# Last chunks, recurrence start and final checks of a convolution-attention-recurrence kernel: matmul before scaling, spread roots, and a hinted branch

## The chip, the cores and the metric

The kernel runs on one core of one Trainium2 chip. The metric is the device time in microseconds (us) of one execution; lower is better. The core's engines each work through their own queue in order: TensorE (PE in the profile, with its weight loads as PEld), VectorE (DVE), ScalarE (ACT), GpSimd (POOL) and SyncE (SP, which here only issues DMAs). They wait for each other through semaphores.

## The reference

The input x has 8 images of 128 channels and 48 x 48 pixels, so 2304 positions. All arithmetic is float32. Two layers are computed:

```
# layer 0: causal attention over the positions
x0 = concat(group_norm(x), position_rows)            # 128 + 32 channels
q, k, v = leaky_relu(W? @ x0 + b?)                   # three times 128 x 2304
x = x + softmax(mask(q.T k / sqrt(128))) v
# layer 1: t = x as tokens, (8, 2304, 128)
n = layer_norm(t);  t = t + softmax(n n.T) n         # full attention
n = layer_norm(t)                                    # over the 128 channels
w = batch_norm(n @ W.T)                              # mean, variance over all 8 * 2304 tokens
y = 0;  for each position: y = sigmoid(w[position] + y @ V.T)
out = t + all the y
```

The batch norm needs every token of all images before the first step of the recurrence. The recurrence is serial over 2304 positions in the reference.

## The kernel before, in words

Positions go through the kernel in chunks of QC = 384, six to an image (`j` = 0 to 5), each of QB = 3 blocks of 128. For every image `b`, class `Causal` computes layer 0's attention and class `Full` layer 1's. `Full` uses that its score matrix is symmetric: a block of exponentials computed for one chunk is turned over by VectorE, stored to DRAM and loaded again for a later chunk (the "turned" products of L1329, from tiles `g`), so that only part of the scores are multiplied out ("direct", L1316 and L1341); the small mirrored ones within a chunk are at L1337.

**How the order is set.** Everything is scheduled by hand. The list `stream` holds all the scores and products in order; each product comes LAG = 3 items behind its score. Beside it a planner (class `Stream`) holds chains of steps. A step is a triple: its function, the TensorE time that it takes, and a list of engine times that says when the next step of its chain falls due; an entry with an empty name is plain waiting time. The planner's clock `now` counts matmul time. After each item `tick` runs at most two steps that are due. A step that needs another chain to be further on forces it with `advance` or `finish`, due or not. So a step's place in each engine's queue follows from these due times, and an engine that reaches a step too early simply waits.

**What follows a chunk of `Full`** (method `after`, L1349): ScalarE copies the chunk's result out of PSUM (`of`, L1361). `residual` transposes it (`of_t`), divides by the softmax sums (`dn`, `ri`), adds the residual into `t2` and computes the token means and variances (`mv`, `ve`). `rooted` has POOL compute the inverse roots. Then there are two ways.

- All chunks but the last two of the last image: the turned `t2` and the turned roots go to DRAM (`spread`), and come back laid out by channel (`fetch`: `t2x` at L1416, and the roots spread over all partitions as `scale` at L1418). `product` keeps `t2x` in `t2c`, multiplies raw `t2x` by the weight `w1T` (L1424), and multiplies the result by the roots (L1425). The weight's rows were centred at the start, so the mean of layer norm needs no subtraction. `stored` copies the result to `wx` (L1430).
- Chunks 4 and 5 of the last image (`last`): `keep_last` transposes `t2` back on TensorE (`tk`, L965) and copies it to `t2c` (L1445); `normed` normalises the tokens on VectorE (L952); `back` transposes them (`tx`) and ScalarE copies them (`xc`, L1460); `statistics` multiplies by `w1T` (L1464), takes statistics (L1469) and copies to `wx` (L1470).

`keep` fills one half of `t2c` with each chunk, and before that forces the chain of the chunk before it; `store` then writes a full `t2c` to DRAM. For chunk 5, `after` also finishes chunk 4's chain and aggregates the statistics so far (L1367). Between these steps `idle` puts matmuls into TensorE's queue whose results nobody reads (L1505); each of its calls is two instructions in the profile.

**The recurrence** (from L1558). The 2304 positions are cut into 96 segments of LS = 24, and all segments of all images run side by side; each starts with WARM = 10 extra steps taken from the segment before, so that its state has converged. The segments form G = 3 groups. Per step and group, TensorE adds `vT_f` times the last state to the input in PSUM tile `z` (L1666), and ScalarE applies the sigmoid (L1667). VectorE makes the inputs two steps at a time as a times wx plus c (`inputs`, L1611, from the batch norm's coefficients `bn_a` and `bn_c`), and the first step's state comes straight from `wx` (L1669). `add_residual` adds `t2` to two steps of states and has SP write them out (L1646, L1647); POOL does it for the second and third group up to a point, VectorE for what is left, and group 0's first 16 steps are written by an accumulating DMA (L1682). The adds' output buffers `rlast` are 8.

**The end.** `seams` (L1632) compares each segment's last state with the state that the next segment's extra steps had reached, `off` says whether any differs too much, and `fl` says whether the attention's scores could have grown too large. A matmul (L1697) and an addition (L1698) make `flag` of both. All engines load it (L1711) and branch (L1712): over `general_path`, the slow and general program, or into it.

Of the kernel before, what the change touches and what calls it, by code (L numbers as in the profile page):

```python
# [14 lines left out]
F32 = mybir.dt.float32  # L15
# [589 lines left out]
def fast_path(ctx: ExitStack, tc: tile.TileContext, x, pe, w_ffn, out, x_tok, w_qkv, w_pos, v_t, gamma_beta, flag):  # L605
# [52 lines left out]
    gb = cpool.tile([P, 2], F32, tag="gb", name="gb")  # L658
    half = cpool.tile([P, 1], F32, tag="half", name="half")
    nc.gpsimd.memset(half, 0.5)  # L660
    v_half = cpool.tile([P, 1], F32, tag="v_half", name="v_half")
    gbv = cpool.tile([P, 1], F32, tag="gbv", name="gbv")

# [7 lines left out]
    with ExitStack() as actx:  # L671
# [16 lines left out]
        def psum_s(name):  # L688
            return ps_s.tile([P, CH], F32, tag="s", name=name)
# [6 lines left out]
        def chunk_tile(tag, name, holder=None, steps=0, bufs=2):  # L696

            if holder is not None:
                before = holders.setdefault(tag, deque([({}, 0)] * bufs))
                old, n = before.popleft()  # L700
                before.append((holder, steps))
                if "chain" in old:
                    st.advance(old["chain"], n)
            return (work if bufs == 2 else work1).tile([P, QC], F32, tag=tag, name=name)
# [245 lines left out]
        def normalize(dst, y, mv, rs):  # L950
            for g in range(QB):
                nc.vector.tensor_scalar(dst[:, ts(g, P)], y[:, ts(g, P)], mv[:, g, 0:1], rs[:, g : g + 1], ALU.subtract, ALU.mult)  # L952
# [7 lines left out]
        def turned_back(src, name):  # L960

            tp = psum_t(name)
            out_ap = tp[:, :QC].rearrange("p (a g r) -> p g a r", a=R, g=QB)
            for g in range(QB):
                nc.tensor.transpose(out_ap[:, g], src[:, ts(g, P)], ident)  # L965
            return tp
# [218 lines left out]
        class Full:  # L1185
# [163 lines left out]
            def after(self, j, o):  # L1349
# [79 lines left out]
                    store()  # L1429
                    nc.scalar.copy(wx[:, :, b, ts(j, SJ)], c["scale"].rearrange("p (s l) -> p l s", l=LS))  # L1430

                def normed():
                    c["x2"] = chunk_tile("t2x", f"x2_{b}_{j}", c, 5, bufs=1)
                    normalize(c["x2"], c["t2"], c["mv"], c["rs"])

                before = self.before.get("chain")

                def keep(t2x):

                    k = j % (SG // SJ)  # L1440
                    if before is not None:
                        st.advance(before, 6 if k else len(before.steps) + before.done)
                    if k == 0:
                        self.t2c = work1.tile([P, LS, SG], F32, tag="t2c", name=f"t2c_{b}_{j}")
                    nc.scalar.copy(self.t2c[:, :, ts(k, SJ)], t2x.rearrange("p (s l) -> p l s", l=LS))  # L1445
# [8 lines left out]
                        nc.sync.dma_start(out[0, :, :LA, b, :], self.t2c[:, :LA])  # L1454
                        nc.sync.dma_start(t2l_d[:, :, b, :], self.t2c[:, LA:])

                def back():
                    tp = turned_back(c["x2"], f"tx_{b}_{j}")
                    c["xc"] = chunk_tile("scale", f"xc_{b}_{j}", c, 6, bufs=1)
                    nc.scalar.copy(c["xc"], tp[:, :QC])  # L1460

                def statistics():
                    tp = psum_t(f"wx_{b}_{j}")
                    nc.tensor.matmul(tp[:, :QC], w1T, c["xc"], start=True, stop=True)  # L1464
                    to = stats[:, b * NQ + j, :]
                    if b == B - 1 and j == NQ - 1:
                        idle(psum_s("idle_last2"), 8)
                        to = most[:, 3:]
                    nc.vector.bn_stats(to, tp[:, :QC])  # L1469
                    nc.scalar.copy(wx[:, :, b, ts(j, SJ)], tp[:, :QC].rearrange("p (s l) -> p l s", l=LS))  # L1470

                def keep_last():
                    keep(turned_back(c["t2"], f"tk_{b}_{j}")[:, :QC])
                    if b == B - 1 and j == NQ - 1:
                        idle(psum_s("idle_last1"), 8)
                    store()

                if last:
                    steps = [
                        (keep_last, 0.35, [("ACT", 0.85)]),  # L1480
                        (normed, 0.0, [("DVE", 1.1)]),
                        (back, 0.35, [("ACT", 0.5)]),
                        (statistics, QC * US, [("DVE", 0.55), ("ACT", 0.85)]),
                    ]
                else:
                    steps = [
                        (turn_root, 0.0, [("DVE", 0.15)]),
                        (spread, 0.0, [("", 13.0)]),
                        (fetch, 0.0, [("", 12.0)]),
                        (product, QC * US, [("DVE", 1.0)]),  # L1490
                        (stored, 0.0, [("ACT", 0.85)]),
                    ]
                c["chain"] = self.before["chain"] = st.add([
                    *through,
                    (residual, 0.0 if far else 0.35, [("DVE", 4.0)]),
                    (rooted, 0.0, [("POOL", 0.9)]),
                    *steps,
                ], max(at, st.free["DVE"]) + 0.2 - st.now)

# [2 lines left out]
        def idle(tp, n):  # L1502

            for _ in range(n):
                nc.tensor.matmul(tp[:, :P], ident, ident, start=True, stop=True)  # L1505
# [57 lines left out]
    with ExitStack() as rctx:  # L1563
# [23 lines left out]
        for t in range(-WARM, -WARM + 2 * TZ, TZ):  # L1587
            for g in range(G):
                z = ps_z[g].tile([P, TZ, B, SG], F32, tag="z", name=f"z_{g}_{t}")
                nc.tensor.matmul(z.rearrange("p t b s -> p (t b s)"), zero[:, :P], zero, start=True, stop=True)  # L1590
                banks[g].append(z)
        idle(pw[:, 2 * P :], 8)

        mv = rc.tile([P, 2], F32, tag="bn_mv", name="bn_mv")
        nc.vector.bn_aggr(mv, most)
# [43 lines left out]

        ys = {}  # L1640

        def add_residual(g, l0, yt):
            engine, pool = (nc.gpsimd, rres) if g and l0 < LM - TZ else (nc.vector, rlast)
            r = pool.tile([P, TZ, B, SG], F32, tag="r", name=f"r_{g}_{l0}")
            t2 = t2s[g].rearrange("p b l s -> p l b s")[:, l0 : l0 + TZ] if g else t2l[:, l0 - LA : l0 - LA + TZ]
            engine.tensor_add(r, yt, t2)  # L1646
            nc.sync.dma_start(out[g, :, l0 : l0 + TZ], r)  # L1647


        nc.tensor.matmul(pw[0:1, :B], ones[:, 0:1], bound, start=True, stop=True)  # L1650
        fl = rc.tile([1, 4], F32, tag="fl", name="fl")
        nc.vector.reduce_max(fl[:, 0:1], pw[0:1, :B], AX.X)
        nc.vector.tensor_scalar(fl[:, 1:2], fl[:, 0:1], LOGIT_BOUND / SCALE, None, ALU.is_gt)
# [32 lines left out]
                    for l0 in range(LA, LM, TZ):  # L1686
                        add_residual(0, l0, ys[0, l0])

        for l0 in range(LM, LS, TZ):
            for g in range(G):  # L1690
                add_residual(g, l0, ys[g, l0])
        for g in range(G):
            seams(g)
        off = rc.tile([P, 1], F32, tag="off", name="off")
        nc.vector.tensor_reduce(off, dm, AX.X, ALU.max)
        nc.vector.tensor_scalar(off, off, STATE_TOL, None, ALU.is_gt)
        nc.tensor.matmul(pw[0:1, P : P + 1], off, ones[:, 0:1], start=True, stop=True)  # L1697
        nc.vector.tensor_scalar(flag, pw[0:1, P : P + 1], fl[:, 1:2], 0.5, ALU.add, ALU.is_gt)  # L1698

@with_exitstack
def conv_attn_hybrid_kernel(ctx: ExitStack, tc: tile.TileContext, args, laid):


    nc = tc.nc
    fpool = ctx.enter_context(tc.tile_pool(name="flag", bufs=1))
    flag = fpool.tile([1, 1], mybir.dt.int32, tag="flag", name="flag")
    x, w_ffn, pe, out = (args[i] for i in (0, 7, 11, 12))
    fast_path(tc, x, pe, w_ffn, out, *laid, flag)  # L1710
    redo = nc.values_load(flag[0:1, 0:1], min_val=0, max_val=1, skip_runtime_bounds_check_because="the flag is the result of a comparison")  # L1711
    with tc.If(redo > 0):  # L1712
        general_path(tc, *args)


# [39 lines left out]
```

## Time and profile before

| what | value |
|---|---|
| three runs | 1713.53, 1719.08 and 1719.97 us; median 1719.08 |
| the profiled execution | 1715.02 us, of which the span from first to last instruction is 1713.3 |
| instructions | 22451 |
| busy in the span | PE 1687.8 us (99%), DVE 1209.1 (71%), ACT 684.8 (40%), POOL 449.9 (26%) |
| mean granted TensorE clock | 0.995 |
| DMA | 291.67 MB, mean 170 GB/s |

Busy times are those of single instructions on the engine; a matmul's end is modelled. The parts that the change touches are all in the last 90 us of the span: the last image's chunks 4 and 5 (from about 1620 us), the coefficients of the batch norm (around 1650 us), the recurrence's 34 steps (to 1698 us) and the end. The profile describes one execution, and the runs are others.

### The profile page before, as it was taken

How to read it: one execution, taken by the hardware profiler on the slowest of the kernel's cores; microseconds unless marked ns; L12 is line 12 of the kernel's file. 1: busy time of each engine (PE TensorE's matmuls, PEld its weight loads, DVE VectorE, ACT ScalarE, POOL GpSimd, SP SyncE). 2: the span in 40 equal slices, each digit the busy share in tenths (PEclk: the TensorE clock that was granted, in tenths of full speed). 3: DMA queues.
4: the chain of work that ended last, by engine and by line, in shares of the span. 5: the costliest groups of instructions: out<-in, count | busy, mean ns of one | idle time of the engine just before them, and what ended most of it. 6: DMA issues, size and time to landing. Idle time of an engine off the chain costs nothing.

```text
span 1713.3 us, 22451 instructions
## 1 busy us (share of the span) xinstructions
PE 1687.8 (99%) x6259; PEld 1085.4 (63%) x6259; DVE 1209.1 (71%) x3297; ACT 684.8 (40%) x1300; POOL 449.9 (26%) x637
## 2 busy tenths in 40 slices
PE   9999999999999999999999999999999999999986
PEld 5666666666666666666666666666666666666665
DVE  5875578666886578865787568865798657974467
ACT  3344334433344324443244333443244442443355
POOL 1233122312133122322124112331213221341205
PEclk9999999999999999999999999999999999999998
DMA  3337763568445774368735684448743686347857
GB/s 122 101 89 210 225 200 109 131 193 251 129 129 145 238 230 128 79 189 244 205 101 130 199 252 139 125 130 244 227 146 71 176 244 207 81 96 211 237 221 223
DMA packets 316731, 291.67 MB, mean 170 GB/s; under 512 B 195793, under 2 KB 280690, under 8 KB 315956
## 3 DMA queue, kind: packets, MB, share of 16 engines
q1 hardware_dynamic: 306572, 268.76, 54.7%
q0 software_dynamic: 9792, 20.99, 4.5%
q8 instruction: 52, 0.85, 0.2%
q14 instruction: 83, 0.68, 0.1%
q10 hardware_dynamic: 232, 0.40, 0.1%
HBM read 164.13 MB, written 125.90 MB: 169 GB/s over the span
## 4 chain that ended last, share of the span: by engine, by line
PE 96%; DMA 2%; DVE 1%; SPq 0%; issue 0%; ACT 0%; DVEq 0%; ACTq 0%
PE s L1038 17%; PE s L1316 17%; PE o L1049 17%; PE o L1341 17%; PE o L1329 13%; PE pj L899 3%; PE pj L902 2%; PE o L1337 2%; PE z L1666 2%; PE wx L1424 2%; DMA g<-e 1%; PE of_t L957 1%; PE pb L847 0%; PE idle_last L1505 0%; DMA x<-in_x_dram 0%; DMA e<-t 0%
## 5 line engine op out<-in xcount | busy, mean ns | idle before, releaser
L1318 ACT ACTIVATE p<-s,shift 128x384 f32<-128x384 f32 (+2 forms) x504 | 274.2, 550 | 535.9 <-PE s L1316 436.8
L1040 ACT ACTIVATE p<-s 128x384 f32<-128x384 f32 (+2 forms) x504 | 229.4, 460 | 400.1 <-PE s L1038 323.6
L1038 PE MATMUL s<-q,k 128*128 128x384 f32 (+2 forms) x1008 | 380.6, 459 | 0.1
L1316 PE MATMUL s<-xh 128*128 128x384 f32 (+2 forms) x1008 | 379.2, 458 | 0.0
L1049 PE MATMUL o<-p,vT 128*128 128x384 f32 (+2 forms) x1008 | 377.5, 456 | 0.0
L1341 PE MATMUL o<-p,xhT 128*128 128x384 f32 (+2 forms) x1008 | 369.1, 456 | 0.0
L1281 DVE STREAM_TRANSPOSE t<-p 128x384 f32<-128x384 f32 x360 | 186.0, 553 | 170.8 <-DMA e<-t 106.3
L1329 PE MATMUL o<-g,xhT 128*128 128x384 f32 x720 | 282.2, 489 | 0.7 <-DMA g<-e 0.7
L1341 PEld LDWEIGHTS o<-p,xhT 128*128 128x128 f32 x1008 | 189.7, 190 | 120.3
L1049 PEld LDWEIGHTS o<-p,vT 128*128 128x128 f32 x1008 | 186.9, 190 | 109.9 <-POOL p L1043 2.0
L1316 PEld LDWEIGHTS s<-xh 128*128 128x128 f32 x1008 | 183.2, 191 | 99.6 <-issue 0.2
L1038 PEld LDWEIGHTS s<-q,k 128*128 128x128 f32 x1008 | 183.4, 190 | 99.0 <-issue 2.2
L1064 DVE TENSOR_TENSOR acc<-acc,p 128x384 f32<-128x384 f32 (+2 forms) x408 | 212.5, 521 | 23.1 <-DVE acc L1064 1.0
L1329 PEld LDWEIGHTS o<-g,xhT 128*128 128x128 f32 x720 | 132.6, 191 | 80.2 <-DMA g<-e 2.2
L1043 POOL TENSOR_TENSOR p<-p,triu 128x128 f32<-128x128 f32 x144 | 71.3, 497 | 356.1 <-ACT p L1040 355.8
L1266 POOL DMA_DIRECT2D gm<-m x192 | 105.3, 555 | 179.1 <-PE s L1316 63.2
L1262 POOL DMA_DIRECT2D m<-tm x48 | 29.9, 623 | 374.5 <-DVE tm L1249 374.5
L1138 POOL TENSOR_SCALAR xhT<-xhT 128x384 f32<-128x384 f32 x48 | 60.5, 1260 | 150.5 <-DVE yt L1150 121.2
L1249 DVE STREAM_TRANSPOSE tm<-p 128x256 f32<-128x256 f32 x96 | 33.9, 366 | 73.1 <-ACT p L1318 72.3
L899 PE MATMUL pj<-xn,wT 128*128 128x384 f32 x192 | 77.9, 488 | 1.5 <-DVE xn L892 1.5
L947 POOL TENSOR_TENSOR rs_c<-ve_c,mhalf 128x3 f32<-128x3 f32 x48 | 48.2, 1004 | 96.1 <-DVE ve_c L941 86.8
L906 DVE TENSOR_TENSOR q<-pj,pb 128x384 f32<-128x384 f32 x48 | 26.6, 554 | 50.1 <-PE pj L899 50.1
(256 smaller groups left out, 1681.1 us busy)
## 6 DMA issues: line engine op xcount, KB each, us to landing
e<-t SPq DMA_DIRECT2D x480, 144.0 KB
g<-e SPq DMA_DIRECT2D x120, 576.0 KB
pb<-posb_d SPq DMA_DIRECT2D x42, 576.0 KB
t1t<-in_x_tok_dram SPq DMA_DIRECT2D x48, 192.0 KB
m<-tm POOLq DMA_DIRECT2D x48, 192.0 KB, 4.3
gm<-m POOLq DMA_DIRECT2D x192, 48.0 KB, 3.8
t_d<-tt SPq DMA_DIRECT2D x184, 48.0 KB
t2x<-t_d SPq DMA_DIRECT2D x46, 192.0 KB
```

What stands on the lines that cost most here:

```text
L899: nc.tensor.matmul(ps[:, :QC], wT[:, j, :], xn, start=True, stop=True)
L1038: nc.tensor.matmul(s[:, off:QC], keys[b][:, ts(m, P)], queries[b, j][:, off:], start=True, stop=True)
L1040: nc.scalar.activation(p[:, off:], s[:, off:QC], AF.Exp, scale=SCALE)
L1043: nc.gpsimd.tensor_mul(p[:, off : off + P], p[:, off : off + P], triu)
L1049: nc.tensor.matmul(o[:, off:QC], vals[b][:, ts(m, P)], p[:, off:], start=first, stop=last)
L1064: nc.vector.tensor_add(a[:, off:], a[:, off:], p[:, off:])
L1266: nc.gpsimd.dma_start(gm[ts(r, SQ)].rearrange("c a q r -> c a (q r)"), d.rearrange("(a c) b f -> b c a f", a=R)[r])
L1281: nc.vector.transpose(t[:, :, :, g, :].rearrange("p b j r -> p j b r"), p.rearrange("p (j b r) -> p j b r", j=QB, b=R))
L1316: nc.tensor.matmul(s[:, off:QC], xh[:, ts(m, P)], xh[:, j * QC + off : (j + 1) * QC], start=True, stop=True)
L1318: nc.scalar.activation(p[:, off:], s[:, off:QC], AF.Exp, bias=shift)
L1329: nc.tensor.matmul(out_ap, xhT[:, QB * i + g, :], p, start=first, stop=last)
L1341: nc.tensor.matmul(o[:, off:QC], xhT[:, what[1], :], p[:, off:], start=first, stop=last)
```

## The change: what it does

1. `keep_last`, `raised`, `statistics` replace `keep_last`, `normed`, `back`, `statistics` for the two last chunks. `raised` multiplies `w1T` by the raw tokens in `t2c`, and ScalarE copies the product (`wr`). `statistics` spreads the three columns of roots over all partitions with three matmuls (a root column, broadcast, as the stationary operand, against the identity), VectorE multiplies product and roots in place and takes the statistics, and ScalarE copies to `wx`. The due times of chunk 4's steps get plain waiting time added: 5.0 us after `rooted`, 3.0 after `keep_last`, 1.0 after `raised`. Chunk 5's `idle` after `keep_last` has 4 calls instead of 8.
2. In chunk 5's `statistics` a sigmoid of one column (`scrap`) is issued before the copy to `wx`.
3. At the recurrence's start the 8 calls of `idle` go, and the matmul for `fl` takes their place, ahead of the coefficients.
4. At the end, the seams and `off` come first; of the six last additions of the residual, two (the last two steps of groups 0 and 1) are made by TensorE, which adds `t2` and the states in PSUM through the identity and leaves a copy to ScalarE; VectorE keeps the other four, one before the flag and three behind it.
5. The flag is inverted. A branch hint is placed on all engines before the flag is loaded, and the branch is written so that skipping `general_path` is the jump.

```diff
 # Full.after: steps of the two last chunks
                     if before is not None:
-                        st.advance(before, 6 if k else len(before.steps) + before.done)
+                        st.advance(before, min(6 if k else 7, len(before.steps) + before.done))
...
+                final = b == B - 1 and j == NQ - 1
+
+                def keep_last():
+                    keep(turned_back(c["t2"], f"tk_{b}_{j}")[:, :QC])
+                    if final:
+                        idle(psum_s("idle_last1"), 4)
+                    store()
+
+                def raised():
+                    tp = psum_t(f"wr_{b}_{j}")
+                    k = j % (SG // SJ)
+                    nc.tensor.matmul(
+                        tp[:, :QC].rearrange("p (l s) -> p l s", l=LS), w1T, self.t2c[:, :, ts(k, SJ)], start=True, stop=True
+                    )
+                    c["wr"] = chunk_tile("scale", f"wr_{b}_{j}", c, 5, bufs=1)
+                    nc.scalar.copy(c["wr"], tp[:, :QC])
 
                 def statistics():
                     tp = psum_t(f"wx_{b}_{j}")
-                    nc.tensor.matmul(tp[:, :QC], w1T, c["xc"], start=True, stop=True)
-                    to = stats[:, b * NQ + j, :]
-                    if b == B - 1 and j == NQ - 1:
+                    by_token = tp[:, :QC].rearrange("p (a g r) -> p g a r", a=R, g=QB)
+                    for g in range(QB):
+                        nc.tensor.matmul(by_token[:, g], c["rs"][:, g : g + 1].to_broadcast([P, P]), ident, start=True, stop=True)
+                    if final:
+                        nc.scalar.activation(scrap, half, AF.Sigmoid)
                         idle(psum_s("idle_last2"), 8)
-                        to = most[:, 3:]
-                    nc.vector.bn_stats(to, tp[:, :QC])
-                    nc.scalar.copy(wx[:, :, b, ts(j, SJ)], tp[:, :QC].rearrange("p (s l) -> p l s", l=LS))
...
+                    z = c["wr"].rearrange("p (l s) -> p l s", l=LS)
+                    nc.vector.tensor_mul(z, tp[:, :QC].rearrange("p (s l) -> p l s", l=LS), z)
+                    nc.vector.bn_stats(most[:, 3:] if final else stats[:, b * NQ + j, :], c["wr"])
+                    nc.scalar.copy(wx[:, :, b, ts(j, SJ)], z)
 
                 if last:
                     steps = [
-                        (keep_last, 0.35, [("ACT", 0.85)]),
-                        (normed, 0.0, [("DVE", 1.1)]),
-                        (back, 0.35, [("ACT", 0.5)]),
-                        (statistics, QC * US, [("DVE", 0.55), ("ACT", 0.85)]),
+                        (keep_last, 0.35, [("ACT", 0.85), ("", 0.0 if final else 3.0)]),
+                        (raised, QC * US, [("ACT", 0.5), ("", 0.0 if final else 1.0)]),
+                        (statistics, 0.35, [("DVE", 1.1), ("ACT", 0.85)]),
                     ]
...
-                    (rooted, 0.0, [("POOL", 0.9)]),
+                    (rooted, 0.0, [("POOL", 0.9), ("", 5.0 if last and not final else 0.0)]),
...
 # recurrence, start
-        idle(pw[:, 2 * P :], 8)
+        nc.tensor.matmul(pw[0:1, :B], ones[:, 0:1], bound, start=True, stop=True)
...
-        nc.tensor.matmul(pw[0:1, :B], ones[:, 0:1], bound, start=True, stop=True)
         fl = rc.tile([1, 4], F32, tag="fl", name="fl")
...
 # recurrence, end
-        for l0 in range(LM, LS, TZ):
-            for g in range(G):
-                add_residual(g, l0, ys[g, l0])
+        def summed(g, l0):
+
+            z = ps_z[g].tile([P, TZ, B, SG], F32, tag="z", name=f"zr_{g}_{l0}")
+            for part, start in ((tokens_of(g, l0), True), (ys[g, l0], False)):
+                nc.tensor.matmul(z, ident, part, start=start, stop=not start)
+            r = rlast.tile([P, TZ, B, SG], F32, tag="r", name=f"r_{g}_{l0}")
+            nc.scalar.copy(r, z)
+            return partial(nc.sync.dma_start, out[g, :, l0 : l0 + TZ], r)
+
+        summed(0, LS - TZ)()
         for g in range(G):
             seams(g)
         off = rc.tile([P, 1], F32, tag="off", name="off")
         nc.vector.tensor_reduce(off, dm, AX.X, ALU.max)
         nc.vector.tensor_scalar(off, off, STATE_TOL, None, ALU.is_gt)
+        store = summed(1, LS - TZ)
         nc.tensor.matmul(pw[0:1, P : P + 1], off, ones[:, 0:1], start=True, stop=True)
-        nc.vector.tensor_scalar(flag, pw[0:1, P : P + 1], fl[:, 1:2], 0.5, ALU.add, ALU.is_gt)
+        for g in range(G):
+            add_residual(g, LM, ys[g, LM])
+            if g == 0:
+                store()
+                nc.vector.tensor_scalar(flag, pw[0:1, P : P + 1], fl[:, 1:2], 0.5, ALU.add, ALU.is_le)
+        add_residual(2, LS - TZ, ys[2, LS - TZ])
 # the branch
-    redo = nc.values_load(flag[0:1, 0:1], min_val=0, max_val=1, skip_runtime_bounds_check_because="the flag is the result of a comparison")
-    with tc.If(redo > 0):
+    tc.mark_branch_hint_location("redo", "LikelyTaken", engines=list(nc.engines))
+    kept = nc.values_load(flag[0:1, 0:1], min_val=0, max_val=1, skip_runtime_bounds_check_because="the flag is the result of a comparison")
+    with tc.If(kept > 0, preferred_fallthrough_block=False, label="redo") as same:
+        pass
+    with same.Else():
         general_path(tc, *args)
```

## The prediction

> **What bounds the kernel now.** I read the page first. TensorE is busy 99% of the 1713.3 us, so in the attention loops only fewer or faster matmuls would help, and the change leaves those loops alone. What can move is the last 90 us, where the order of small steps decides. I went there with the timeline, then the waits, then the instructions of the branch.
>
> Waits from 1625 to 1656 us (engine and line, what it waited for: total, times, longest):
>
> ```profile
> PE wx L1424 <- DMA t2x<-t_d: 4.0, 1, 4.0
> ACT L1669 <- DVE bn_cv L1602: 1.3, 1, 1.3
> DVE fl L1652 <- PE pw L1650: 1.2, 1, 1.2
> ```
>
> The first is TensorE standing still in the last chunk of attention; the others sit at the start of the recurrence. The timeline (start, duration, engine, line, operation) gives the places:
>
> ```profile
> 1631.37 1.14 ACT L1445 COPY t2c<-t2x 128x384 f32<-128x384 f32 x1 [4.98 <-DMA t2x<-t_d]
> ...
> 1639.36 1.43 DVE L1367 BATCH_NORM_AGGREGATE most<-stats 128x2 f32<-128x282 f32 x1
> ...
> 1641.82 0.56 DVE L1376 TENSOR_REDUCE dn<-of_t 128x3 f32<-128x384 f32 x1 [0.78 <-PE of_t L957]
> ...
> 1644.74 0.49 PE L965 MATMUL tk<-ident,t 128*128 128x128 f32 x3
> ...
> 1649.63 0.20 DVE L1595 BATCH_NORM_AGGREGATE bn_mv<-most 128x2 f32<-128x9 f32 x1
> ...
> 1651.38 1.28 ACT L1669 ACT_TABLE_LOAD   x1 [1.32 <-DVE bn_cv L1602]
> ...
> 1654.44 0.80 DVE L1620 TENSOR_SCALAR z_-8_14609<-wx,bn_a,bn_c 128x512 f32<-128x512 f32 x1
> ```
>
> These rows are the milestones that I cost: t2x lands, `dn` starts the final residual, `bn_mv` closes the statistics, and the second input tile (`z_-8`) starts. After 1656.81 TensorE repeats every 0.43 us with no wait, so the recurrence shifts as a block with that tile. Its last sigmoid ends at 1698.06. What follows is 15.2 us of tail:
>
> ```profile
> 1704.67 0.21 DVE L1698 TENSOR_SCALAR flag<-pw,fl 1x1 int32<-1x1 f32 x1 [0.28 <-PE pw L1697]
> ```
>
> and, from the lists of instructions of lines 1712 and 1751 (times in ns, first and last start in us):
>
> ```profile
> L1712 PEldq COMPARE_BRANCH  x1: 3462/3462/3462, 1705.5 to 1705.5; - x1
> L1712 SPq EVENT_SEMAPHORE  x8: 17/17/17, 1709.2 to 1709.8; - x8
> L1751 POOLq DRAIN  x3: 46/107/2685, 1709.7 to 1713.0; - x3
> ```
>
> The flag is ready at 1704.88, all engines branch by 1705.6, none does anything before 1709.0, and GpSimd's 2.69 us drain comes last.
>
> **What the skill says.** "Runtime: NRT & Kernel Launch", section "Instruction fetch mechanics": a taken branch to a page outside the fetched window must wait for a DMA of that page. The 3.46 us above agrees. "ScalarE: Activation LUTs", "What ACT_TABLE_LOAD costs": about 1283 ns plus a drain of 1380 ns. Here the load takes 1.28 us and the sigmoid starts at 1652.67 directly behind it; no drain shows. "TensorE: Matmul & The Clock Gate", "What's actually happening": an idle window of about 3.4 us halves the clock. Here the 4.0 us stall is followed by a granted clock of 0.54 from 1633.0 to 1636.5, with products 0.64 us apart instead of 0.32.
>
> **Step 1, chunk 4 of the last image.** `keep_last` forces chunk 3's `product`, in whose matmul TensorE waits for t2x. `rooted` now gives 5 us more before it. The products behind that place are seven turned ones (0.645 us each), chunk 5's own scores and product (0.21 each) and one mirrored (0.22), 5.2 us: `keep_last` comes out one product before the end, and the stall goes. But t2x is fetched when t_d has landed (1625.9), untouched, so it still lands at 1631.37, and ScalarE's queue now decides. TensorE reaches chunk 3's matmul about 1633.0 (turned products wait some 0.4 us for their tile) and ends it at 1633.7. VectorE's product takes 0.56, and ScalarE's strided copy 1.14 (wx<-scale): 1635.6. The t2c store, next in line with about 2.4 us, lands earlier, at 1635.0. Then come copy tk 0.48 (1636.1), the raw product 0.9 cold (1637.05), the spread roots as three fp32 matmuls of 0.244 each (16 half ones of L1505 take 1.95 us) and 0.17 latency (1637.85), multiply 0.60, bn_stats 0.60 (1639.05), the aggregate 1.43 and two small ones 0.25: `dn` at 1640.8 instead of 1641.82. **Gain 1.0**, though the stall and slow clock were over 5 us. SP's order around the fetch does not change. The final o copy sits behind copy tk, ending at 1636.6, under this cover.
>
> **Step 2, final chunk.** `dn` to the root's end took 4.30 (1646.12) and stays. Then came normalise, transpose, copy, matmul, bn_stats: 3.51 until 1649.63. Now three spreads 1.0 with hops, multiply 0.60, bn_stats 0.65: 2.25. **Gain 1.25.** The raw product must be there first: t2 at `dn`+1.9, transposes 0.4, four idle calls 0.98 (ScalarE's copy beside them), product 0.8, copy 0.55 make `dn`+4.6; the multiply waits until `dn`+5.3. The 14 idle calls (3.4) end at 1641.7, ahead of t2 at 1642.7; now they delay tk by a microsecond.
>
> **Step 3, into the recurrence.** Scrap's sigmoid loads the table ahead of wx's copy, under VectorE's multiply and statistics; the first sigmoids follow `bn_cv` at once. The flag's matmul moves before the coefficients and eight idle calls (1.95) go, so VectorE passes `fl` in 0.3 us rather than waiting: from `bn_mv` to `z_-8` 3.67 instead of 4.81. **Gain 1.15.** ScalarE's own gain (1.3) and TensorE's (over 2) are larger, so VectorE decides. Together the recurrence starts 3.4 us sooner. The t2s loads start 1.8 sooner too, since tk does; POOL's adds and their outputs shift as one.
>
> **Step 4, tail**, in the old frame, before the shift. Six adds of 0.60 and a 0.45 wait preceded the seams. Now VectorE starts them at 1697.3; 2.6 us and two small ones give `off` at 1700.3. TensorE's four residual products, 512 columns or 0.853 each (twice z's 0.43), end at 1701.05, and the flag's matmul queues behind. Flag: 1701.5, not 1704.88. ScalarE's two copies (about 0.6) hide. Three of VectorE's adds remain behind the flag, to 1703.35, so SP issues its last write at 1703.4, 1.5 later than before, and branches at 1704.3, not 1705.46. POOL, idle, branches near 1702 and drains under this. The hint stands behind each engine's last work, so SP arms it only 0.5 us ahead: target at 1707.45 for 1709.22. Its semaphores take 1.42 as before, then 0.9 of barrier: 1709.8 for 1713.26. **Gain 3.45.**
>
> Sum: 1.0 + 1.25 + 1.15 + 3.45 = **6.9 us**. The profiled execution took 1715.02 (span 1713.3 plus 1.7), giving 1708.1. But the three runs lie at 1713.53, 1719.08 and 1719.97; the median of these four is 1717.05, which I take: **1710**.
>
> **Costs not shown.** A weight load with stride zero: nothing if like other loads (0.19), up to 0.5 if element fetch slows it; a better layout might gain 0.1; I take zero. The multiply reads PSUM at stride 24: L1470's ScalarE copy reads so at 0.48 without penalty; VectorE's could cost 0 to 0.6 (its contiguous z, unlike scale, could save ScalarE 0.66, off the path); I take zero. The hint: lost, minus 0.5; perfect, plus 2.5; its own instruction 0 to 0.1.
>
> **Rivals.** (A, 0.43) The sum above, 3.9 to 9.9. (B, 0.40) The target is there when the engines branch. SP's part would end near 1705.7; then the last write, issued 1703.4 and landing about 2.4 later like the t2c store, binds, with 1.4 of semaphores and barrier: 1707.2. Gain 9.4, **1707.6**. For it: five engines fetched in the same 4 us before and now arrive spread out. Against: SP's half microsecond. (C, 0.12) The wait only moves: t2c's store lands later or the strided multiply is slow, steps 1 and 2 give nothing, and a late write eats 1 us of the tail: gain 3.5, **1713.5**. This includes that the hint does nothing. (D, 0.05) Slower: TensorE is short of filler. It now idles from 1634.0 to 1636.2, 1.2 us before tk, and again around the roots; should the clock be half as the recurrence starts, each step costs 2.58 rather than 1.29. Six steps eat the gain; 16 steps give **1731**. Against: each gap is under the 4.0 that halved it before.
>
> **How the numbers follow.** A measurement here tells about 0.5% from no change, 8.6 us. B lies beyond it almost wholly (0.38), A by two fifths (0.17), C not: faster 0.55, same 0.40, slower 0.05. A's and B's spread and the base (1715 to 1719) give 1703; C sets 1716.
>
> **What would show it.** Right: no wait of TensorE for t2x near 1631, `dn` near 1640.8, the table load before `bn_mv`, `bn_mv` to `z_-8` under 3.8, flag 3.4 after the last sigmoid. Wrong: `dn` past 1641.8; a clock of half past `bn_mv`; SP's first semaphore behind the branch under 1 us (B) or 3.7 us after it (no hint). A recurrence pace other than 0.43 would overturn the sum.

## The result and the profile after

| what | before | after |
|---|---|---|
| median of 22 runs | 1716.55 us (1711.96 to 1721.94) | 1709.76 us (1707.72 to 1714.95) |
| the profiled execution, its span | 1715.02, 1713.3 us | 1714.05, 1712.0 us |

The ratio of the times is 0.9966, with a 95% interval from 0.9956 to 0.9977: 3.9 to 7.6 us less, by the medians 6.8, by the means 6.2. The forecast was 1710.0. That is faster, but by less than the 0.5% that the forecast set as its bound.

The two profiled executions differ by only 1.0 us. The one after is already 6.6 us later when chunk 4 of the last image starts its final residual (`dn` at 1628.03 instead of 1621.43 us), before any instruction that the change touches. In its trace TensorE's granted clock is 0.50 from 10.2 to 23.9 us, where that of before is 1.00. Executions of one kernel differ by as much: eleven of after's 22 lie from 1707.7 to 1709.1 us at a mean granted clock of 0.998 or 0.999, the other eleven from 1710.4 to 1715.0 at 0.997 or less. So single times say little here. I compare the stretches behind chunk 4's `dn`, each within its own trace. L is the end of the recurrence's last sigmoid.

| stretch, us | before | after | gain | predicted gain |
|---|---|---|---|---|
| `dn` of chunk 4 to `dn` of chunk 5 | 20.39 | 18.44 | 1.95 | 1.0 |
| that to `bn_mv` | 7.81 | 6.64 | 1.17 | 1.25 |
| `bn_mv` to the second input tile | 4.81 | 3.54 | 1.27 | 1.15 |
| that to L | 43.62 | 43.62 | 0 | 0 |
| L to the last instruction | 15.19 | 11.71 | 3.48 | 3.45 |
| sum | 91.82 | 83.95 | 7.9 | 6.9 |

Outside the span it gave back 0.3 (more under the hardware findings).

The first row may overstate what the change did. t2x, whose fetch the change leaves alone, landed 9.94 us behind chunk 4's `dn` in before (1631.37) and 8.46 behind it in after (1636.49). The table under "Edit 1 alone" compares the stretch at like landings: about 0.55 us are left of the 1.95.

The waits of after from 1628 to 1660 us (engine and line, what it waited for: total, times, longest). The 4.0 us of TensorE for t2x and VectorE's 1.2 for `fl` are gone. What is left of the first is a shorter wait in ScalarE's queue, and one of TensorE behind it:

```profile
PE wr L1465 <- ACT t2c L1442: 1.6, 1, 1.6
ACT t2c L1442 <- DMA t2x<-t_d: 1.4, 1, 1.4
```

The timeline of after (start, duration, engine, line, operation, count, idle time before it and its releaser), with the milestones of before in the same order:

```profile
1636.49 1.13 ACT L1442 COPY t2c<-t2x 128x384 f32<-128x384 f32 x1 [1.42 <-DMA t2x<-t_d]
...
1640.70 0.91 PE L1465 MATMUL wr<-t2c,w1T 128*128 128x384 f32 x2 [1.61 <-ACT t2c L1442]
...
1644.88 1.43 DVE L1368 BATCH_NORM_AGGREGATE most<-stats 128x2 f32<-128x282 f32 x1
...
1646.47 0.55 DVE L1377 TENSOR_REDUCE dn<-of_t 128x3 f32<-128x384 f32 x1
...
1647.97 0.76 PE L966 MATMUL tk<-ident,t 128*128 128x128 f32 x3 [0.81 <-DVE t L1386]
...
1650.81 1.28 ACT L1477 ACT_TABLE_LOAD   x1
...
1653.12 0.20 DVE L1600 BATCH_NORM_AGGREGATE bn_mv<-most 128x2 f32<-128x9 f32 x1
...
1656.65 0.80 DVE L1625 TENSOR_SCALAR z_-8_14601<-wx,bn_a,bn_c 128x512 f32<-128x512 f32 x1
```

The reader is to see three things. `dn` follows VectorE's aggregate at once, with no wait of its own: VectorE now sets it. The table load has moved ahead of `bn_mv`. And TensorE still stood for 1.61 us ahead of the raw product (L1465), without losing its clock.

The tail: the flag, then the branches and the drains (minimum, median and longest in ns, first and last start in us), and last the hints:

```profile
1703.45 0.20 DVE L1717 TENSOR_SCALAR flag<-pw,fl 1x1 int32<-1x1 f32 x1 [0.38 <-PE pw L1712]
```

```profile
L1733 SPq EVENT_SEMAPHORE  x8: 17/17/17, 1707.2 to 1710.3; - x8
L1733 ACTq COMPARE_BRANCH  x1: 68/68/68, 1704.5 to 1704.5; - x1
...
L1733 PEldq COMPARE_BRANCH  x1: 5026/5026/5026, 1704.6 to 1704.6; - x1
```

```profile
L1774 POOLq DRAIN  x3: 46/109/2678, 1705.2 to 1711.7; - x3
...
L1774 PEldq BRANCH_PREFETCH_HINT  x1: 50/50/50, 0.9 to 0.9; - x1
```

The flag is ready at L + 3.38, as predicted. But the hint is not executed behind each engine's last work: it is executed on all engines at 0.8 to 0.9 us after the start. ScalarE is past the branch at once (its next semaphore comes at 1705.0), TensorE is not: it takes 5.03 us, until 1709.6. And SP, which waits for the writes, is done only at 1710.3; the last write landed at L + 9.46 = 1709.7. TensorE's jump and the last write thus ended within about 0.1 us of each other.

### The profile page after: what moved, and what is told of

Same layout as the page of the kernel before. It is cut to its first block, busy times and chain, and to the rows that moved or that the text cites. A ratio compares the mean times of both kernels' runs of the same rounds, so it can differ in the third digit from the quotient of the medians.

```text
span 1712.0 us, 22440 instructions
## 1 busy us (share of the span) xinstructions
PE 1695.4 (99%) x6249; PEld 1088.5 (64%) x6249; DVE 1207.4 (71%) x3291; ACT 687.1 (40%) x1303; POOL 451.4 (26%) x637
## 4 chain that ended last, share of the span: by engine, by line
PE 95%; DMA 2%; DVE 1%; SPq 1%; issue 0%; POOL 0%; ACT 0%; DVEq 0%; POOLq 0%; ACTq 0%
PE s L1039 17%; PE s L1317 17%; PE o L1050 17%; PE o L1342 17%; PE o L1330 12%; PE pj L900 3%; PE z L1673 2%; PE pj L903 2%; PE o L1338 2%; PE wx L1425 2%; DMA g<-e 1%; PE of_t L958 1%; DMA e<-t 1%; PE pb L848 1%; PE dn L1098 0%; PE pb L851 0%
```

## The experiments

All are single executions with a trace, except the last, which was timed nine times. The tail comes first, since there the predicted size was hit with steps that were not what happened.

### The tail: hint, order, branch

**Hint alone.** The kernel before with edit 5 only:

```diff
+    tc.mark_branch_hint_location("redo", "LikelyTaken", engines=list(nc.engines))
-    with tc.If(redo > 0):
-        general_path(tc, *args)
+    with tc.If(kept > 0, preferred_fallthrough_block=False, label="redo") as same:
+        pass
+    with same.Else():
+        general_path(tc, *args)
```

> The kernel before with the inverted flag and the hinted branch alone. Measured from the end of the last sigmoid: before, flag ready at 6.8 us and end at 15.2; changed kernel, 3.4 and 11.7. Theory 1 (the hint removes the fetch on four engines, TensorE still fetches, so with an unchanged flag at 6.8 the end is flag + 0.6 load + 3.5 to 5 fetch + 1.0 barrier): end at 12.0 to 13.5. Theory 2 (the earlier flag made the gain, the hint none): end at 15.2. If TensorE is hinted too: GpSimd's drain of 2.7 binds, end at 11.5.

**No hint.** The kernel after, with the branch and the flag of before (the same diff the other way round).

> The changed kernel with the old unhinted branch and old sense of the flag. Theory 1: SP branches 6.4 us after the last sigmoid, fetches for 3.7 to 5, then 1.4 of semaphores and 0.85 of barrier: end at 12.4 to 13.7 after the last sigmoid (11.7 with the hint). Theory 2 (the order gave the whole gain): 11.7. Theory 3 (the hint gave the whole gain): 15.2.

**No branch.** The kernel after without `general_path`, the load of the flag and the branch; this part of the program is left out.

> The changed kernel without general_path, the load of the flag and the branch: the fallback is left out. Theory 1a (the last write's landing, 9.9 us after the last sigmoid, binds): end at 11.4 to 11.7 after the last sigmoid. Theory 1b (TensorE's fetch of 5.0 binds, and the instruction fetches slow the writes): landing at 8 and end at 9.5 to 10.5.

| us after L | flag | last write issued | landed | end |
|---|---|---|---|---|
| before | 6.81 | 3.85 | 7.46 | 15.19 |
| hint alone | 6.70 | 3.90 | 7.25 | 11.44 |
| no hint | 3.38 | 5.21 | 9.89 | 12.21 |
| after (both) | 3.38 | 5.21 | 9.46 | 11.71 |
| no branch | 3.38 | 5.21 | 7.40 | 9.23 |

The branch in the kernel with the hint alone (list of instructions of its line):

```profile
L1713 SPq EVENT_SEMAPHORE  x8: 17/17/17, 1703.2 to 1703.8; - x8
...
L1713 PEldq COMPARE_BRANCH  x1: 491/491/491, 1702.7 to 1702.7; - x1
```

Here no engine waits for instructions: all go on about 0.5 us after the branch, and GpSimd's drain binds, the last case of the expectation (11.5). Without the hint the end lies 0.2 us below theory 1's range. Without the branch theory 1b had the direction, but both landing and end came earlier than it said. The hint alone is worth 3.75 us and the new order alone 2.98, but together they give 3.48. They are substitutes: the hint takes the fetch out of the way behind the flag; the order brings the flag ahead of the writes, which makes the writes the end. With the writes last, the hint has little left to save, 0.5 us.

Without the branch the same writes, issued at the same 5.21, land 2.06 us sooner. The two traces in the stretch from L + 7 to L + 9 (columns: busy time of PE, PEld, DVE, ACT, POOL, then TensorE's clock, DMA share, GB/s), after and then no branch:

```profile
1707.27:1708.27 1.00, 0.00 (x0) 0.00 (x0) 0.00 (x0) 0.00 (x0) 0.00 (x0) 0.50 0.45 145
1708.27:1709.27 1.00, 0.00 (x0) 0.00 (x0) 0.00 (x0) 0.00 (x0) 0.00 (x0) 0.50 0.13 45
```

```profile
1701.37:1702.37 1.00, 0.00 (x0) 0.00 (x0) 0.00 (x0) 0.00 (x0) 0.00 (x0) 0.50 0.26 98
1702.37:1703.37 1.00, 0.00 (x0) 0.00 (x0) 0.00 (x0) 0.00 (x0) 0.00 (x0) 0.50 0.04 8
```

In after a thin rest of the writes drags on. In that time its DMA view shows instruction fetches (the queues of kind "instruction", packets and MB, from 1705 to 1711 us), where the kernel without a branch has one on q14:

```profile
q8 instruction: 2, 0.03, 2.6%
q14 instruction: 4, 0.03, 1.6%
```

"Runtime: NRT & Kernel Launch" in the Trainium skill, section "Instruction fetch mechanics", says that a jump to a page outside the fetched window waits for a DMA of that page. TensorE's 5.03 us agree, and the fetch is a DMA like the writes. That engines which jump at L + 4.3 slow the writes through their fetches is argued from this coincidence. What is shown is that the load of the flag and the branch, taken out together, cost those writes 2 us.

**Why TensorE missed.** The kernel after, with 16 tiny matmuls put into TensorE's queue near the start, whose results nobody reads, so that its branch stands elsewhere in its stream of instructions:

```diff
+        fill = psum_s("fill")
+        for _ in range(16):
+            nc.tensor.matmul(fill[0:1, 0:1], ident[:, 0:1], ident[:, 0:1], start=True, stop=True)
```

> The changed kernel with 16 tiny matmuls more in TensorE's queue, in a wait near the start of the kernel. After the last sigmoid: TensorE's branch takes 5.0 us at 4.3, the last write lands at 9.5, the end is at 11.7. Theory 1 (TensorE's branch stands short of the end of a page of instructions, so its hinted target isn't fetched ahead; 64 instructions more put a page's end some 5 us ahead of the branch): the branch takes 0.5, no fetch of 16384 bytes on that queue between 2 and 8 us, the last write lands near 8, end at 9.8 to 10.4. Theory 2 (the hint is lost on TensorE here for another reason): branch 5.0, end 11.7.

Its branch row:

```profile
L1736 PEldq COMPARE_BRANCH  x1: 491/491/491, 1702.0 to 1702.0; - x1
```

0.49 instead of 5.03 us: where the branch stands in the stream of instructions turned it. In after, q8 (the instruction queue with fetches of 16384 bytes, which I take for TensorE's) had no fetch from 25 us before L until L + 6.45; here it has one at L - 0.87 and the next at L + 6.33. All kernels with the hint fit this: the five whose TensorE branch took 0.49 us have such a fetch 0.7 to 3.0 us before L; in the three at about 5 us the last one lies 19 to 25 us before it. Why a recent fetch helps isn't shown.

Theory 1 held for the branch and not for the rest: the end came only 0.29 sooner, at L + 11.42 instead of 9.8 to 10.4, since the last write still landed at L + 9.21 and not near 8. So TensorE's miss was nearly hidden, and the writes bind.

**One addition to GpSimd.** The kernel after, with one of VectorE's last adds given to the idle GpSimd:

```diff
-        for g in range(G):
+        for g in range(2):
             add_residual(g, LM, ys[g, LM])
...
+        nc.gpsimd.tensor_add(r2, ys[2, LM], tokens_of(2, LM))
```

> The changed kernel with one of VectorE's additions behind the flag (group 2, LM) given to GpSimd, which is idle then, and written first. Theory 1a (the last write's landing binds): the last write is issued 0.6 us sooner, and the end comes 0.4 to 0.6 sooner, 11.1 to 11.3 after the last sigmoid, where TensorE's fetch binds. Theory 1b (TensorE's fetch binds): end unchanged at 11.7. Rival (GpSimd's addition slows VectorE's seams by sharing SBUF access): flag later than 3.4, end at 12 or more.

```profile
1697.08 1.74 POOL L1706 TENSOR_TENSOR r_LM<-y,t2s 128x512 f32<-128x512 f32 x1 [0.56 <-ACT y L1674]
1697.61 2.36 DVE L1654 TENSOR_TENSOR r<-y,t2l 128x512 f32<-128x512 f32 x2
```

The two adds that VectorE makes beside it take 2.36 us; in after the same group takes 1.28. The seams move back, the flag comes at L + 3.96 and the end at L + 11.96, 0.25 later than in after. Neither form of theory 1 came, but the rival: work given to GpSimd was not free for VectorE.

**Writes first.** From all this a better order: all six adds and their writes ahead of the last group's seams, `off` and the flag, with hint and filler.

```diff
-        summed(0, LS - TZ)()
+        for g in range(G):
+            add_residual(g, LM, ys[g, LM])
+        summed(0, LS - TZ)()
+        summed(1, LS - TZ)()
+        seams(0)
+        seams(1)
+        add_residual(2, LS - TZ, ys[2, LS - TZ])
+        seams(2)
```

> The kernel after with the 16 tiny matmuls, and with all six last additions and their writes issued before the seams of group 2, off and flag. Theory 1 (the instruction fetches of the branching engines slow writes that are under way, and the last landing sets the end): flag 5.0 to 5.5 us after the last sigmoid, last write issued by 2.5 and landed by 7.0, the end 9.7 to 10.3 after the last sigmoid and set by the flag, with GpSimd's drain behind it; 1.3 us less than with the tiny matmuls alone (11.42). Theory 2 (the writes take as long whatever the order, or the fetches come earlier with the hint's target): landed after 8.5, end 11 or more.

Flag at L + 5.26, last write issued at 4.09 and landed at 7.55, end at 10.13. Theory 1 held for the flag and the end. The write was issued 1.6 later than I had put it, behind the seams of the first two groups and VectorE's add, and so landed half a microsecond past its bound. The drain row starts at 1704.8 and, 2.68 us long, ends at 1707.5; SP's semaphores of the branch are done at 1706.2:

```profile
L1735 SPq EVENT_SEMAPHORE  x8: 17/17/17, 1704.7 to 1706.2; - x8
```

```profile
L1776 POOLq DRAIN  x3: 46/109/2678, 1704.8 to 1708.0; - x3
```

Now GpSimd's drain behind the flag sets the end, and no longer a write. Against after that is 1.58 us, against the kernel with the tiny matmuls alone 1.29.

### The last chunks and the start of the recurrence

**No waiting times.** The kernel after with the plain waiting times of edit 1 at zero:

```diff
-                        (keep_last, 0.35, [("ACT", 0.85), ("", 0.0 if final else 3.0)]),
+                        (keep_last, 0.35, [("ACT", 0.85), ("", 0.0)]),
...
-                    (rooted, 0.0, [("POOL", 0.9), ("", 5.0 if last and not final else 0.0)]),
+                    (rooted, 0.0, [("POOL", 0.9), ("", 0.0)]),
```

> The changed kernel with the three plain waiting times (5.0, 3.0 and 1.0 us in the planner) put to zero. Measured from chunk 4's dn to chunk 5's dn: before 20.4 us, changed kernel 18.4. Theory 1 (the waiting times keep TensorE from standing in front of t2x and then of chunk 4's t2c): two stalls of 2 to 4 us each ahead of the last products, 22 to 24 us. Theory 2 (the chain behind t2x's landing on ScalarE and VectorE decides wherever the steps stand): 18.4 to 19.9.

Its timeline:

```profile
1632.21 0.88 PE L1425 MATMUL wx<-t2x,w1T 128*128 128x384 f32 x2 [3.90 <-DMA t2x<-t_d]
...
1636.22 1.65 PE L1465 MATMUL wr<-t2c,w1T 128*128 128x384 f32 x2 [2.28 <-ACT t2c L1442]
```

Both stalls, and the product takes 1.65 instead of 0.91 us: the granted clock is 0.50 from 1636 to 1640. `dn` to `dn` takes 23.68, 3.3 more than before, and t2x landed at the same place (9.88 behind `dn`, 9.94 in before). So the raw product without the waiting times would have lost; they take the loss away.

**Table load alone.** The kernel before with edit 2, the sigmoid of one column:

```diff
                     if b == B - 1 and j == NQ - 1:
+                        nc.scalar.activation(scrap, half, AF.Sigmoid)
                         idle(psum_s("idle_last2"), 8)
```

> The kernel before with the early sigmoid of one column (scrap) alone. From bn_mv to the end of the last sigmoid: before 48.4 us, changed kernel 47.2. Theory 1 (VectorE decides, which still waits for the flag's matmul behind eight idle calls): 48.4, no gain, though the table load leaves the place in front of the first sigmoid. Theory 2 (the table load of 1.28 was on the path): 47.2.

The load moves ahead of `bn_mv` (1648.21 against 1649.85), and `bn_mv` to the second input tile stays 4.81. VectorE waits 1.18 us for the flag's matmul, and that decides:

```profile
1654.39 0.15 DVE L1654 TENSOR_REDUCE fl<-pw 1x1 f32<-1x8 f32 x1 [1.18 <-PE pw L1652]
```

**Flag's matmul alone.** The kernel before with edit 3 only:

```diff
-        idle(pw[:, 2 * P :], 8)
+        nc.tensor.matmul(pw[0:1, :B], ones[:, 0:1], bound, start=True, stop=True)
...
-        nc.tensor.matmul(pw[0:1, :B], ones[:, 0:1], bound, start=True, stop=True)
```

> The kernel before with the flag's matmul in the place of the eight idle calls at the recurrence's start, alone. From bn_mv to z_-8: before 4.81 us, changed kernel 3.54; to the end of the last sigmoid 48.4 and 47.2. Theory 1: z_-8 at 3.5 to 3.7, but ScalarE's first sigmoids still stand behind the table load, so that the recurrence gains 0.6 to 0.9: 47.5 to 47.8. Theory 2 (VectorE alone decides): 47.2. If the clock suffers from the missing idle calls: over 48.4.

3.54 us instead of 4.81, and then 43.74 instead of 43.62 to L: 1.16 of the 1.27, and the table load is worth the remaining 0.1. So VectorE decides here, as predicted, and the late table load costs next to nothing.

The tail of this kernel, with before's code, took 13.98 us instead of 15.19: the flag came 0.56 sooner, and SP went on 3.2 us behind its branch, not 3.7 as in before or 3.9 and 4.0 in the kernels with edit 1 or 2 alone. Why is not known. The sizes of hint and order above, from one trace each, are to be read with such a microsecond in mind.

**Edit 1 alone.** The kernel before with edit 1 and nothing else.

> The kernel before with edit 1 alone (raw product, spread roots, waiting times, four filler calls less); the table load, the flag's matmul, the tail and the branch stay as before. Theory 1 (edits 1 to 3 act on separate stretches and add up): chunk 4's dn to chunk 5's dn 18.4 to 19.5 us, dn to bn_mv 6.6 to 6.7, bn_mv to the second input tile 4.81, last sigmoid to the end 15.2; in all 2.1 to 3.1 us less than before from chunk 4's dn to the end. Theory 2 (what the earlier statistics give is taken back, since the eight filler calls and the flag's matmul then stand in front of the coefficients and TensorE reaches them no sooner): bn_mv to the second input tile 5.5 us or more, and 1.5 us or less in all.

`dn` to `dn` 18.44 and `dn` to `bn_mv` 6.64, both as in after; `bn_mv` to the second tile 4.15, and the end at L + 15.13. Neither theory had that 4.15, nor the sum: 3.8 us less than before, over theory 1's 3.1. TensorE's fillers are done earlier against `bn_mv`, and VectorE's wait for `fl` shrinks from 1.2 to 0.5 us:

```profile
DVE fl L1655 <- PE pw L1653: 0.5, 1, 0.5
```

So edits 1 and 3 overlap: edit 3 gives 1.16 alone, but 0.61 behind edit 1 (4.15 to 3.54).

The kernels above repeat the stretch from `dn` to `dn` with the code of before or that of after, and show what else moves it. t2x has landed when ScalarE's copy to `t2c` starts:

| kernel | code of the stretch | t2x landed, us behind `dn` | `dn` to `dn` |
|---|---|---|---|
| hint alone | before's | 8.03 | 17.30 |
| table load alone | before's | 9.56 | 20.01 |
| flag's matmul alone | before's | 9.75 | 20.20 |
| before | before's | 9.94 | 20.39 |
| after, no hint, edit 1 alone, 16 tiny matmuls, writes first | after's | 8.39 to 8.48 | 18.44 |
| addition on GpSimd | after's | 9.34 | 19.24 |
| no branch | after's | 9.44 | 19.34 |

From the kernel with the hint alone, then from the one with no branch:

```profile
1630.00 0.88 PE L1424 MATMUL wx<-t2x,w1T 128*128 128x384 f32 x2 [2.04 <-DMA t2x<-t_d]
...
1639.16 0.56 DVE L1376 TENSOR_REDUCE dn<-of_t 128x3 f32<-128x384 f32 x1 [0.78 <-PE of_t L957]
```

```profile
1630.68 1.14 ACT L1442 COPY t2c<-t2x 128x384 f32<-128x384 f32 x1 [2.40 <-DMA t2x<-t_d]
...
1640.58 0.55 DVE L1377 TENSOR_REDUCE dn<-of_t 128x3 f32<-128x384 f32 x1
```

With a late landing, before's code takes 10.45 us from there to `dn` (three traces, TensorE's clock halved behind the stall) and after's 9.90 (two traces, full clock): edit 1 gains 0.55. With the early landing of the kernel with the hint alone, TensorE stood for 2.04 us and kept its clock, and before's code was 1.1 us faster than after's ever was. The mean is 19.5 for the four with before's code and 18.7 for the seven with after's. Whether the change itself makes t2x land sooner isn't shown: both codes have early and late landings.

**Spread and aggregate sooner.** The kernel after with the filler, chunk 4's roots spread right behind its raw product, and the aggregate over the chunks before it moved up (over 46 chunks instead of 47; chunk 4's statistics then join the last aggregate):

```diff
                     nc.scalar.copy(c["wr"], tp[:, :QC])
+                    if not final:
+                        spread_roots()
...
-                    nc.vector.bn_aggr(most[:, 1:3], stats[:, : B * NQ - 1, :])
...
+                    else:
+                        nc.vector.bn_aggr(most[:, 1:3], stats[:, : B * NQ - 2, :])
```

> The kernel after with 16 tiny matmuls near the start, chunk 4's roots spread right behind its raw product instead of a step later, and the aggregate over the earlier chunks (46 instead of 47, so that it doesn't wait for chunk 4) made at chunk 4's keep_last. Theory 1 (VectorE's aggregate of 1.43 us and two small instructions, with the wait for the spread roots, stand between chunk 4's statistics and dn of chunk 5): chunk 4's dn to chunk 5's dn 16.2 to 17.2 us instead of 18.44, all later stretches within 0.1 of the kernel after, the end 1.3 to 2.2 us sooner. Theory 2 (dn waits for TensorE's transposed result of chunk 5, which comes in its own time): 18.0 us or more, no gain.

`dn` to `dn` 16.99, within the range of theory 1: VectorE's queue was what held `dn`. But `dn` to `bn_mv` rises to 6.97. The 14 filler calls (28 instructions) did not move up with `dn`; `tk` stands behind them and starts 2.9 us after `dn` (1.5 in after), as in the kernel without waiting times, which has the same 6.97. Of 1.45 gained, 1.1 remains:

```profile
1643.28 3.29 PE L1517 MATMUL idle_last<-ident 128*128 128x128 f32 x28
1643.48 0.56 DVE L1374 TENSOR_REDUCE dn<-of_t 128x3 f32<-128x384 f32 x1 [1.20 <-PE of_t L958]
...
1646.41 0.49 PE L966 MATMUL tk<-ident,t 128*128 128x128 f32 x3
```

**All together,** the kernels "writes first" and "spread and aggregate sooner" joined.

> The two runs before this one joined: roots of chunk 4 spread sooner, aggregate sooner, writes first, tiny matmuls. Theory 1 (the two stretches add up): 3 to 4 us below the kernel after, 9.5 to 11 below the kernel before, ratio to before about 0.994. Theory 2 (one of the two gives nothing): 5.5 to 8.5 us below before, ratio 0.995 to 0.997.

Median 1709.72 us of nine runs (1705.33 to 1710.92), before, timed beside it, 1715.08: ratio 0.9960, interval 0.9947 to 0.9974. That is theory 2's size, 5.4 us, and not told apart from after's 0.9966. The tail came as wanted, end at L + 10.11. But in the profiled run `dn` to `dn` took 18.91, not 16.99. Its timeline shows a large part of why, and beside it that of the kernel with spread and aggregate sooner:

```profile
1638.88 1.38 PE L1472 MATMUL wr<-t2c,w1T 128*128 128x384 f32 x2 [1.98 <-ACT t2c L1439]
...
1640.05 1.48 PE L1467 MATMUL wx<-ident,roots 128*128 128x128 f32 x6
```

```profile
1639.44 0.91 PE L1472 MATMUL wr<-t2c,w1T 128*128 128x384 f32 x2 [1.83 <-ACT t2c L1439]
...
1640.19 0.83 PE L1467 MATMUL wx<-ident,roots 128*128 128x128 f32 x6
```

ScalarE's copy to `t2c` waited 0.27 us for the store of t2s, which it did not in the other kernel; TensorE stood still 1.98 us instead of 1.83, and the granted clock behind the stall fell to 0.62 and then 0.50 where the other kept 1.00. The length of the stall alone doesn't decide this. TensorE stood for 2.04 us in the kernel with the hint alone (above) and for 2.03 in the one with the addition on GpSimd, and both kept 1.00:

```profile
1640.03 0.91 PE L1465 MATMUL wr<-t2c,w1T 128*128 128x384 f32 x2 [2.03 <-ACT t2c L1442]
```

What else decides, and how often the clock was lost in the executions without a trace, isn't known. So I can't offer the joined kernel as a proven better one.

## Why the prediction was right or wrong

**The number** came out within 0.3 us, at rival A, the sum. Its base held too: the median of four executions, 1717.05, against 1716.55 of 22. Taking the profiled execution alone would have given 1708.1. That the sum fits so well is in part luck, as steps 1 and 4 show.

**Step 1** was right that TensorE's stall for t2x goes: none of the seven kernels with after's code has it. Its size, 1.0, is not confirmed. The two traces give 1.95, but the working had t2x land untouched at 1631.37, and it landed 1.48 us sooner behind `dn` in after. From the landing to `dn` the working had 9.43 us (1631.37 to 1640.8); at late landings it was 9.90, a gain of 0.55 on before's 10.45. "`keep_last` comes out one product before the end" failed: it came out three products earlier than counted. I had counted the planner's clock as running with the products. But ahead of the mirrored product the code calls `finish` for the chain that brings the mirrored blocks back (L1311 of after), and `finish` sets the clock to that chain's due time, almost 5 us on, so that `keep_last`, not yet due by the products, became due at once. That fits the 1.61 us stall of TensorE ahead of the raw product, which I hadn't seen coming. And the "ScalarE's queue decides" of the working became, at the very end, VectorE's: the aggregate ends and `dn` starts (1644.88 + 1.43 = 1646.31; `dn` at 1646.47). That the waits matter is shown: without the waiting times the stretch takes 3.3 us longer than in before, at a like landing.

**Step 2**, 1.17 for 1.25, and **step 3**, 1.27 for 1.15, were right as worked, but for one point: the 14 idle calls did not delay `tk`, which waited 0.81 us for t2; they do once `dn` comes sooner (16.99, above). That VectorE decides in step 3 is shown by edits 2 and 3 alone. Both costs that I took as zero behaved so: the multiply at stride 24 took 0.56 us, as `scale`'s contiguous one does, and the spread roots 0.83 for the three.

**Step 4** hit 3.45 with 3.48 for a wrong reason. Its parts: the flag at 3.4 after L was right (3.38). "SP arms it only 0.5 us ahead" was wrong, since the hint runs at the start. SP had no fetch to wait for: its first semaphore came 0.5 us behind its branch (1706.7 to 1707.2), in before 3.7 (1705.5 to 1709.2). In place of A's 3.2 us for the target SP waited for the last write, which is rival B's mechanism. But B priced the landing at 2.4 us after the issue and 1.4 from there to the end; in after it took 4.25 (5.21 to 9.46) and 2.24, and in the kernel with no branch 2.19 and 1.83. Nor was B's target there for every engine: TensorE's jump ended at L + 9.33, so that quick writes alone would not have given B's 9.4 us. So two errors of A cancelled: the hint worked on SP, and the write that the new order had put last landed as late as A's target (L + 9.46; A's 1707.45 is L + 9.39).

**Rivals C and D** did not come as such: in after t2c's store and the multiply cost nothing, and the pace from the second tile to L is 43.62 us in both traces. C's late write did come, within step 4.

## What to carry to other kernels

Before summing gains in a tail, ask for each what binds once it is there: an early flag and a hinted branch each removed the same wait, and behind both stood a write that the new order had itself put last. Issue what must land (the writes) first, and what only decides (the flag) behind it. In a hand-made schedule, undo the waiting times on their own: here they stand between a loss of 3.3 us and a small gain. And where a transfer's landing falls into a stretch, compare traces with like landings: one trace of each kernel showed 1.95 us where at a like landing 0.55 is left.

## What the runs showed of the hardware

- A branch hint was executed 0.8 us after the start of the span on every engine (TensorE 0.9), though the program places it ahead of the flag's load, and a hinted jump 1700 us later still took only 0.5 us on TensorE (3.46 without, kernel before). It missed there in three kernels (5.03, 4.99 and 5.04 us) and hit in five (0.49), and 16 tiny matmuls near the start were enough to turn it. Without a hint the same split shows: 3.40 to 3.46 us in the three kernels with a fetch on q8 within 1.5 us before L, 4.48 and 4.82 in the two whose last one lay 20 us before it.
- The time outside the span is 2.07 to 2.18 us in seven of the eight kernels with a hint (1.81 in the one with the add on GpSimd), and 1.71 to 1.85 in the others. The cause was not looked for; it takes 0.3 us off what the hint gives.
- An add of 128x512 on GpSimd (1.74 us) stretched VectorE's adds beside it, 2.36 us for two instead of 1.28.
- The Trainium skill's "TensorE: Matmul & The Clock Gate", "What's actually happening", puts the idle window at about 3.4 us. Here a clock of one half followed a single stall of 1.98 us (all together), and did not follow stalls of 2.03 (addition on GpSimd), 2.04 (hint alone), 1.83 or 1.61. The length of the stall alone doesn't tell.
